# Experts stage of a two-layer metaformer: block 0's second product taken directly, and the row index worked out in block 4 instead of block 2

## The chip, the cores and the metric

The kernel runs on one core of one Trainium2 chip. Its time is the device time of one execution in microseconds (us); the time before is 2829.91 us, the median of three runs (2828.95 to 2830.11). All data is float32 unless a profile row says otherwise.

## The reference

Two layers run on 4 images of 32x32 tokens with 384 channels. Layer 0 is an attention and a mixture of experts; layer 1 is a local "outlook" attention and a feed-forward net with factored weights. The change lies in the mixture of experts:

```python
scores = jnp.einsum('bsd,de->bse', x, gate_w) + gate_b
probs = jax.nn.softmax(scores, axis=-1)
topk_vals, topk_idx = jax.lax.top_k(probs, TOP_K)      # 2 of 4 experts
...
h = jax.nn.gelu(jnp.einsum('bsd,edh->ebsh', x, w1) + b1[:, None, None, :], approximate=False)
y = jnp.einsum('ebsh,ehd->ebsd', h, w2) + b2[:, None, None, :]
out = jnp.einsum('bse,ebsd->bsd', masked, y)
```

Here x is the normed token, w1 is 384x1536 and w2 is 1536x384 for each expert. The kernel computes only the two chosen experts of each token.

## The kernel before

There are 4096 tokens and so 8192 pairs of a token and an expert. They are sorted by expert through a table in DRAM and worked in 35 blocks: blocks 0 to 3 of 256 tokens (`NFIRST` = 4), whose tokens come from the first three images, so that they can start before the last image is routed; then three short blocks, 4 to 6, of 128 tokens (`NHALF`); then blocks 7 to 34 of 256 tokens (`NLEAD` = 7 is the first of them). Every block has one expert; which expert and which tokens is worked out on the chip.

**One block** (loop at L1669). At its start GpSimd (POOL) is given the fetch of the next block's weights (`weights`, L1576: `up` of 128x4620, `down` of 128x4992) and tokens (`fetch`, L1600). There are two places for weights, so a load waits until the block two back has let go of its weights. TensorE makes 12 hidden tiles (L1693: 3 matmuls each, weights `up`, into a PSUM tile `ps_h`, three of which exist), and ScalarE takes the gelu of each (L1698). The order of hidden tiles is 0, 1, 2, 6, 7, 8, 3, 4, 5, 9, 10, 11. Then VectorE norms the next block's tokens (`norm`, L1609), and the second product follows.

**The second product** has two forms. A short block takes the direct one: 12 accumulated matmuls of 128x384 (L1715), one addition of the bias (L1720), one store of `y` to `yg`. (A float32 matmul shows as two rows of the profile, so the rows count 24.) A whole block cuts the 256x1536 by 1536x384 product into quadrants and makes it of seven products of half size instead of eight. For that VectorE makes four sums of quarters of the weights (`folded`, L1643 to L1649, at the block's start) and four sums of quarters of h (`paired`, L1656 to L1659, tiles `hsum`), one group after the hidden tile 8 and one after 11, that is after the sixth and the last of the order. The seven products (L1735) go to `ps_y` (three PSUM tiles) and are put together by nine additions of 128x192 (L1739). The third product is the first that reads `hsum`; the fourth needs a PSUM tile again. In both forms the next block's tokens are transposed on TensorE (`turn`, L1619, copied by L1620) ahead of the last part of the second product.

**What runs beside the blocks.** `beside` is a generator; each `next` puts one piece of other work into the instruction streams. It first projects the last image of the attention, one of its 8 tiles a step (L288 on TensorE, then on VectorE the addition of the residual at L760 and statistics at L763 and L764, and the store of x1 at L765; the next tile's residual load, L742, is issued ahead of it by SP, into one of two places). Then it routes that image (13 steps, with a Sqrt at L783 and an Exp at L1303 on ScalarE, and the scatter into the table on POOL at L1373), and then it runs `schedule`, L1447 on: which blocks there are, the rows of weights and tokens of all blocks (`self.all`, L1508, which blocks 4 and later need), and after that the index: where in `yg` the two results of each token lie (L1510 to L1531). The index is read by `gather` (L1540), first in block 18, where the adding up of results begins.

Steps are taken after a hidden tile's gelu: six in block 0 (those of the tiles with f % 6 >= 3), twelve each in blocks 1 and 2; what is left is taken at the start of block 3. Thus block 0 has projections 1 to 6, block 1 has projections 7 and 8 and routing, and block 2 has the end of routing (steps 19 and 20), `schedule`'s first three pieces (21 to 23), the two loops for the index (24, ahead of the first hsum group) and its last part (25, ahead of the second).

**What sets the order.** The instructions of TensorE, VectorE, ScalarE and SP stand in the order in which the program writes them (`manual_schedule`), each engine works its own list in order, and an engine that waits holds all that is behind. POOL's list is ordered by the framework's scheduler. After block 34 the outlook stage begins, whose work follows in the same lists.

Of the kernel before, what the change touches and what calls it, by code (L numbers as in the profile page):

```python
# [17 lines left out]
P = 128  # L18
# [1196 lines left out]
class Router:  # L1215
# [10 lines left out]
    def __init__(self, net, pool, keep, psum):  # L1226
        self.net, self.nc, self.tc, self.pool, self.psum = net, net.nc, net.tc, pool, psum
        nc = self.nc
        self.NJ = NT * P // XB

        def const(name, shape, dtype=FP):
            return pool.tile(shape, dtype, name=f"rt_{name}")

        def count(t, pattern, base=0, step=0):
            nc.gpsimd.iota(
                t, pattern=pattern, base=base, channel_multiplier=step, allow_small_or_imprecise_dtypes=True
            )

        self.ones = const("ones", [P, P])
        nc.gpsimd.memset(self.ones, 1.0)  # L1240
        self.before = const("before", [P, P])
        nc.gpsimd.affine_select(
            out=self.before, in_=self.ones, compare_op=ALU.is_ge, fill=0.0,
            base=-1, pattern=[[1, P]], channel_multiplier=-1,
        )
        self.lower, self.upper = const("lower", [P, NE, NE]), const("upper", [P, NE, NE])
        count(self.lower, [[1, NE], [-1, NE]])
        nc.vector.tensor_scalar(self.upper, self.lower, -0.5, None, ALU.is_lt)
        nc.vector.tensor_scalar(self.lower, self.lower, 0.5, None, ALU.is_gt)
        self.steps = const("steps", [P, self.NJ])  # L1250
        count(self.steps, [[XB, self.NJ]])
        self.number = const("number", [P, NXB])
        count(self.number[:, :NFIRST], [[UNITS, NFIRST]])
        count(self.number[:, NFIRST:NLEAD], [[1, NHALF]], base=UNITS * NFIRST)
        count(self.number[:, NLEAD:], [[UNITS, NXB - NLEAD]], base=UNITS * NFIRST + NHALF)
        self.lane = const("lane", [P, 1])
        count(self.lane, [[0, 1]], step=1)
        self.region = const("region", [P, NE])
        count(self.region, [[NT * P, NE]])

        self.next = const("next", [P, B + 2, NE])
        nc.gpsimd.memset(self.next, 1.0)
        nc.gpsimd.memset(self.next[:, :, 0:1], -float(NE - 1))
        nc.gpsimd.memset(self.next[:, 0, 0:1], 0.0)

        self.at = const("at", [P, NT, NE])
        self.sel = const("sel", [P, NT, NE])
        self.slot = [const(f"slot_{n}", [P, NT]) for n in range(2)]
        self.upto = const("upto", [P, B + 1, NE])
        nc.gpsimd.memset(self.upto[:, 0, :], 0.0)  # L1270
        self.index = [keep.tile([P, NT], mybir.dt.int32, name=f"index_{n}", tag=f"index_{n}") for n in range(2)]
        self.weight = [keep.tile([P, NT], FP, name=f"weight_{n}", tag=f"weight_{n}") for n in range(2)]
        none = const("none", [P, self.LINE], mybir.dt.int32)
        nc.gpsimd.memset(none, 0)
        n = NE * NT
        nc.sync.dma_start(
            out=net.table.rearrange("(t p) w -> p t w", p=P), in_=none.unsqueeze(1).to_broadcast([P, n, self.LINE])
        )
# [267 lines left out]
def experts(net, router, x1, x2, wup, wdown, beside):  # L1546
# [12 lines left out]
    with ExitStack() as ctx:  # L1559
# [53 lines left out]
        def turn(n):  # L1613
            xb = xbs.pop(n)
            xbT = halves[n % 2].tile([P, KC, XB], FP, name="xbT", tag="xbT")
            for t in range(tiles(n)):
                ps = router.psum()
                for c in range(KC):
                    nc.tensor.transpose(ps[:, c * P : (c + 1) * P], xb[:, t, c * P : (c + 1) * P], net.ident)  # L1619
                nc.vector.tensor_copy(  # L1620
                    xbT[:, :, t * P : (t + 1) * P], ps[:, :C].rearrange("p (c t) -> p c t", c=KC)
                )
            return xbT
# [44 lines left out]
        xbT = turn(0)  # L1668
        for n in range(NXB):  # L1669
            if n == NFIRST - 1:  # L1670
                for _ in beside:
                    pass
            if n + 1 < NXB:
                if n + 1 >= NFIRST:
                    tokens(n + 1)
                ws[n + 1] = weights(n + 1)
                fetch(n + 1)
            store()
            store = lambda: None
            if n > router.complete(added // NB):  # L1680
                store = add(added)
                added += 1
            up, down = ws.pop(n)
            size = tiles(n) * P
            whole = size == XB
            if whole:
                w11, w21, w22, t1, t2, t3, t4, shift = folded(down)
            hs, ss = [None] * NG3, []
            for f in (*range(0, 3), *range(6, 9), *range(3, 6), *range(9, 12)):
                ps = ps_h.tile([P, XB], FP, name="ps_h", tag="h")[:, :size]  # L1690
                for k in range(KC):
                    o = k * HID + f * P
                    nc.tensor.matmul(  # L1693
                        ps, lhsT=up[:, o : o + P], rhs=xbT[:, k, :size], start=k == 0, stop=k == KC - 1,
                    )
                if f % 3 == 0:
                    hs[f // 3] = hp.tile([P, 3, XB], FP, name="h", tag="h")
                nc.scalar.activation(  # L1698
                    hs[f // 3][:, f % 3, :size], ps, AF.Gelu, bias=up[:, KC * HID + f : KC * HID + f + 1]
                )  # L1700
                if n < NFIRST - 1 and (n or f % 6 >= 3):
                    next(beside, None)
                if whole and f in (8, 11):
                    g = len(ss)
                    ss.append(paired(hs[g], hs[g + 2], g))
            if n + 1 < NXB:
                norm(n + 1)
            else:
                net.scale(0, added)
            if not whole:  # L1710
                if n + 1 < NXB:
                    xbT = turn(n + 1)
                ps = ps_y.tile([P, C], FP, name="ps_y", tag="y")
                for f in range(NF):
                    nc.tensor.matmul(  # L1715
                        ps, lhsT=hs[f // 3][:, f % 3, :size], rhs=down[:, f * C : (f + 1) * C],
                        start=f == 0, stop=f == NF - 1,
                    )
                y = work.tile([P, C], FP, name="y0", tag="y0", bufs=2)
                nc.vector.tensor_tensor(y, ps, down[:, NF * C :], ALU.add)  # L1720
                nc.sync.dma_start(out=net.yg[first_row(n) : first_row(n + 1), :], in_=y)
                continue
            ys = [work.tile([P, C], FP, name=f"y{t}", tag=f"y{t}", bufs=2) for t in range(TT)]
            (c11, c12), (c21, c22) = ((y[:, :D], y[:, D:]) for y in ys)

            def a(c, t):
                return [hs[f // 3 + 2 * c][:, f % 3, t * P : (t + 1) * P] for f in range(HF)]

            def s(i):
                return [ss[f // 3][:, i, f % 3, :] for f in range(HF)]  # L1730

            def product(left, right):
                ps = ps_y.tile([P, C], FP, name="ps_y", tag="y")[:, :D]
                for f in range(HF):
                    nc.tensor.matmul(ps, lhsT=left[f], rhs=right[:, f, :], start=f == 0, stop=f == HF - 1)  # L1735
                return ps

            def total(out, one, two):
                nc.vector.tensor_tensor(out, one, two, ALU.add)  # L1739

            def send(t):
                nc.sync.dma_start(
                    out=net.yg[first_row(n) : first_row(n + 1), :].rearrange("(p t) c -> p t c", t=TT)[:, t, :],
                    in_=ys[t],
                )

            total(c21, product(a(0, 0), w11), down[:, NF * C : NF * C + D])
            total(c11, product(a(1, 0), w21), c21)
            total(c22, product(s(0), t1), shift)
            total(c21, product(s(1), t2), c21)  # L1750
            total(c12, c21, c22)
            total(c12, product(s(3), w22), c12)
            send(0)
            if n + 1 < NXB:
                xbT = turn(n + 1)
            total(c21, product(s(2), t3), c21)
            total(c22, c21, c22)
            total(c21, product(a(1, 1), t4), c21)
            send(1)
# [606 lines left out]
```

## Time and profile before

| | |
|---|---|
| median of three runs | 2829.91 us |
| profiled execution | 2827.02 us, its span 2825.3 us |
| TensorE matmul (PE) | 2615.5 us busy, 93% of the span |
| VectorE (DVE) | 1720.6 us, 61% |
| ScalarE (ACT) | 1203.6 us, 43% |
| GpSimd (POOL) | 413.8 us, 15% |
| mean granted TensorE clock | 0.959 |
| hidden tiles of the experts, L1693 | 531.8 us busy, first at 1211.6, last at 2250.2 us |
| seven products, L1735, with wsum and hsum | 205.4 us busy, 22.8 us idle before them |
| nine additions, L1739, 128x192 from PSUM | 357 ns each |

A row of a timeline gives the start, the length, the engine, the line, the operation with what it writes and reads, how many instructions are merged, and in brackets how long the engine was idle before it and what ended that. A row of merged matmuls includes the drain of the last, so the start of the next row, not the sum, tells when TensorE was free. In a row of the costliest groups, busy time and mean length in ns stand after the first bar, and idle time before the group and its releaser after the second. PEld is the load of a matmul's stationary operand, and SPq a DMA issue of SP.

### The profile page before, as it was taken

How to read it: one execution, taken by the hardware profiler on the slowest of the kernel's cores; microseconds unless marked ns; L12 is line 12 of the kernel's file. 1: busy time of each engine (PE TensorE's matmuls, PEld its weight loads, DVE VectorE, ACT ScalarE, POOL GpSimd, SP SyncE). 2: the span in 40 equal slices, each digit the busy share in tenths (PEclk: the TensorE clock that was granted, in tenths of full speed). 3: DMA queues.
4: the chain of work that ended last, by engine and by line, in shares of the span. 5: the costliest groups of instructions: out<-in, count | busy, mean ns of one | idle time of the engine just before them, and what ended most of it. 6: DMA issues, size and time to landing. Idle time of an engine off the chain costs nothing. (4 is left out here: it accounts for less than half of the span.)

```text
span 2825.3 us, 40024 instructions
## 1 busy us (share of the span) xinstructions
PE 2615.5 (93%) x14703; PEld 1570.2 (56%) x14703; DVE 1720.6 (61%) x4382; ACT 1203.6 (43%) x2023; POOL 413.8 (15%) x501
## 2 busy tenths in 40 slices
PE   6889998999999997687999999999999988999988
PEld 3323333333333332167899999999999944444432
DVE  1377777677778787657245444655555566877742
ACT  3778777678768876312222212112112122122225
POOL 1000000030003003213211112222221101100000
PEclk9999999999999998789999999999999999999999
DMA  5143434222323242453655455565665447554432
GB/s 106 31 106 90 110 92 129 75 66 72 90 60 75 68 108 58 125 204 125 248 229 208 167 208 209 210 230 210 217 224 203 156 148 217 173 178 149 147 109 91
DMA packets 215804, 404.11 MB, mean 143 GB/s; under 512 B 83344, under 2 KB 176848, under 8 KB 202544
## 3 DMA queue, kind: packets, MB, share of 16 engines
q1 hardware_dynamic: 184496, 187.82, 22.3%
q0 software_dynamic: 26960, 209.05, 21.5%
q10 hardware_dynamic: 4144, 4.61, 0.5%
q8 instruction: 118, 1.93, 0.3%
q14 instruction: 86, 0.70, 0.1%
HBM read 304.34 MB, written 49.00 MB: 125 GB/s over the span
## 5 line engine op out<-in xcount | busy, mean ns | idle before, releaser
L1698 ACT ACTIVATE h<-ps_h,up 128x256 f32<-128x256 f32 (+1 forms) x420 | 195.1, 465 | 839.7 <-PE ps_h L1693 838.8
L1693 PE MATMUL ps_h<-xbT,up 128*128 128x256 f32 (+1 forms) x2520 | 531.8, 372 | 2.5 <-ACT h L1698 1.8
L689 DVE CUSTOM_DVE_ANT_0 e<-e,rz,inv 128x1024 f32<-128x1024 f32 x384 | 475.2, 1274 | 44.6 <-DMA rz<-r_row 44.3
L1693 PEld LDWEIGHTS ps_h<-xbT,up 128*128 128x128 f32 x2520 | 463.1, 191 | 64.5 <-ACT h L1698 2.6
L637 ACT ACTIVATE e<-ps_s,ten 128x1024 f32<-128x1024 f32 x384 | 408.1, 1110 | 64.8 <-PE ps_s L627 33.1
L627 PE MATMUL ps_s<-q,k 32*128 32x512 f32 x1536 | 295.2, 673 | 44.7 <-ACT e L637 31.4
L645 PE MATMUL ps_o<-e,wv 128*32 128x512 f32 x1536 | 226.1, 663 | 50.9 <-DVE wv L696 49.4
L1735 PE MATMUL ps_y<-wsum,hsum 128*128 128x192 f32 x1152 | 205.4, 332 | 22.8 <-DVE hsum L1656 19.6
L645 PE MATMUL ps_z<-e,rt_ones 128*32 128x512 f32 x1536 | 218.3, 642 | 0.0
L716 POOL DMA_DIRECT2D q<-po x96 | 76.1, 877 | 951.5 <-DMA q<-po 560.9
L373 ACT ACTIVATE below<-tk_left,tk_bound 128x1024 bf16<-128x1024 f32 (+1 forms) x160 | 184.4, 1152 | 52.6 <-DVE tk_bound L379 40.4
L1735 PEld LDWEIGHTS ps_y<-wsum,hsum 128*128 128x128 f32 x1152 | 190.9, 193 | 27.3 <-DVE hsum L1656 21.3
L627 PEld LDWEIGHTS ps_s<-q,k 32*128 32x128 f32 x1536 | 92.5, 193 | 182.2 <-ACT e L637 90.2
L1862 PE MATMUL ps_a<-wa,xnT 128*128 128x486 f32 x384 | 169.5, 589 | 9.2 <-DVE attn L1872 7.5
L1739 DVE TENSOR_TENSOR y<-ps_y,y 128x192 f32<-128x192 f32 x160 | 57.2, 357 | 172.0 <-PE ps_y L1735 168.8
L645 PEld LDWEIGHTS ps_o<-e,wv 128*32 128x32 f32 x1536 | 31.4, 112 | 212.5 <-DVE wv L696 64.5
L288 PE MATMUL ps_t<-xnT,wqkv 128*128 128x512 f32 x288 | 135.1, 609 | 2.4 <-ACT xnT L470 1.7
L1735 PE MATMUL ps_y<-down,h 128*128 128x192 f32 x768 | 130.0, 326 | 0.0
L1735 PEld LDWEIGHTS ps_y<-down,h 128*128 128x128 f32 x768 | 126.6, 190 | 1.9
L1862 PEld LDWEIGHTS ps_a<-wa,xnT 128*128 128x128 f32 x384 | 72.3, 194 | 95.2 <-issue 85.5
L645 PEld LDWEIGHTS ps_z<-e,rt_ones 128*32 128x32 f32 x1536 | 52.2, 117 | 131.0 <-issue 127.5
L1540 POOL DMA_INDIRECT yt<-yg,index x64 | 76.7, 1198 | 323.0 <-DVE x L1835 135.3
(392 smaller groups left out, 3539.2 us busy)
## 6 DMA issues: line engine op xcount, KB each, us to landing
band<-room SPq DMA_DIRECT2D x32, 1560.0 KB
rz<-r_row SPq DMA_DIRECT2D x48, 512.0 KB
yg<-y SPq DMA_DIRECT2D x67, 192.0 KB
q<-q SPq DMA_DIRECT2D x192, 64.0 KB
k<-k SPq DMA_DIRECT2D x192, 64.0 KB
room<-none SPq DMA_DIRECT2D x64, 192.0 KB
x<-x SPq DMA_DIRECT2D x35, 192.0 KB
o<-in_x_dram SPq DMA_DIRECT2D x33, 192.0 KB
```

The lines of the kernel that those rows point to most:

```text
L288: nc.tensor.matmul(ps, lhsT=lhsT(k), rhs=rhs(k), start=k == 0, stop=k == KC - 1)
L373: nc.scalar.activation(junk[:n], left[:n], AF.Sign, bias=bound[:n], accum_out=over[:n])
L627: nc.tensor.matmul(ps[:, half * 512 : half * 512 + 512], lhsT=self.k4[r, u * P : (u + 1) * P], rhs=self.q4[r, :], start=True, stop=True,)
L637: nc.scalar.activation(e, ps, AF.Exp, bias=shift, scale=QK_SCALE)
L645: nc.tensor.matmul(ps[r : r + 32, :], lhsT=lhsT(odd), rhs=self.es[2 * u + odd][:, half * 512 : half * 512 + 512], start=u == 0, stop=u == ...
L689: nc.vector.tensor_tensor_reduce(self.es[m], self.es[m], self.rz, 1.0, self.im["inv"][:, m, self.h : self.h + 1], ALU.mult, ALU.add, self. ...
L716: nc.gpsimd.dma_start(out=there, in_=po[r : r + 32, :], accum_op=ALU.add)
L1540: self.nc.gpsimd.indirect_dma_start(out=y, out_offset=None, in_=self.net.yg[: first_row(self.complete(i // NB)), :], in_offset=bass.Indire ...
L1693: nc.tensor.matmul(ps, lhsT=up[:, o : o + P], rhs=xbT[:, k, :size], start=k == 0, stop=k == KC - 1,)
L1698: nc.scalar.activation(hs[f // 3][:, f % 3, :size], ps, AF.Gelu, bias=up[:, KC * HID + f : KC * HID + f + 1])
L1735: nc.tensor.matmul(ps, lhsT=left[f], rhs=right[:, f, :], start=f == 0, stop=f == HF - 1)
L1862: nc.tensor.matmul(pa[:, hh, :HW_], lhsT=xnT[:, k, :], rhs=wa[:, k, hh * HW_ : (hh + 1) * HW_], start=k == 0, stop=k == KC - 1,)
```

## The change

Block 0 is no longer "whole": it takes the direct product, now written for any number of 128-token tiles, with the next block's transposes ahead of the last tile. `folded` and `paired` aren't called for it. The steps of `beside` in blocks 0 to 2 are taken only while `router.all` is not there; the start of block 3 completes the steps up to it if need be; the remaining steps are taken in the short blocks, one after each hidden tile, and what is left at the start of block 7. The line numbers of functions behind the first hunk move by one, in the loop by more.

```diff
+        self.all = None
...
         for n in range(NXB):
             if n == NFIRST - 1:
+                while router.all is None:
+                    next(beside)
+            if n == NLEAD:
                 for _ in beside:
                     pass
...
-            whole = size == XB
+            whole = size == XB and n > 0
...
-                if n < NFIRST - 1 and (n or f % 6 >= 3):
+                if NFIRST <= n < NLEAD or router.all is None and n < NFIRST - 1 and (n or f % 6 >= 3):
                     next(beside, None)
...
+            out = net.yg[first_row(n) : first_row(n + 1), :].rearrange("(p t) c -> p t c", t=tiles(n))
             if not whole:
-                if n + 1 < NXB:
-                    xbT = turn(n + 1)
-                ps = ps_y.tile([P, C], FP, name="ps_y", tag="y")
-                for f in range(NF):
-                    nc.tensor.matmul(
-                        ps, lhsT=hs[f // 3][:, f % 3, :size], rhs=down[:, f * C : (f + 1) * C],
-                        start=f == 0, stop=f == NF - 1,
-                    )
-                y = work.tile([P, C], FP, name="y0", tag="y0", bufs=2)
-                nc.vector.tensor_tensor(y, ps, down[:, NF * C :], ALU.add)
-                nc.sync.dma_start(out=net.yg[first_row(n) : first_row(n + 1), :], in_=y)
+                for t in range(tiles(n)):
+                    if t == tiles(n) - 1 and n + 1 < NXB:
+                        xbT = turn(n + 1)
+                    ps = ps_y.tile([P, C], FP, name="ps_y", tag="y")
+                    for f in range(NF):
+                        nc.tensor.matmul(
+                            ps, lhsT=hs[f // 3][:, f % 3, t * P : (t + 1) * P], rhs=down[:, f * C : (f + 1) * C],
+                            start=f == 0, stop=f == NF - 1,
+                        )
+                    y = work.tile([P, C], FP, name=f"y{t}", tag=f"y{t}", bufs=2)
+                    nc.vector.tensor_tensor(y, ps, down[:, NF * C :], ALU.add)
+                    nc.sync.dma_start(out=out[:, t, :], in_=y)
                 continue
```

## The prediction

> **What bounds the kernel now.** I read the page first, then the waits of the experts stage (1211 to 2251 us), then the timelines of TensorE and VectorE around each long wait. TensorE is busy for 93% of the span, so only its gaps, or its work itself, can give time. In the costliest groups one expert row stands out by its idle time:
>
> ```profile
> L1735 PE MATMUL ps_y<-wsum,hsum 128*128 128x192 f32 x1152 | 205.4, 332 | 22.8 <-DVE hsum L1656 19.6
> ```
>
> In the stage's waits (who waited, for whom: total, times, longest) TensorE waits for hsum three times, and VectorE itself waits for residual loads:
>
> ```profile
> PE ps_y L1735 <- DVE hsum L1656: 18.4, 3, 9.8
> ...
> DVE o L760 <- DMA o<-in_x_dram: 17.2, 4, 9.2
> ```
>
> First gap, block 0, TensorE and then VectorE. The seven products begin at 1241.67, and 6.65 us pass until hsum is there. The groups of hsum are not slow: VectorE stood 9.21 us ahead of them for the residual tile of the sixth projection.
>
> ```profile
> 1241.67 4.06 PE L1735 MATMUL ps_y<-down,h 128*128 128x192 f32 x24
> 1245.57 1.14 PE L1735 MATMUL ps_y<-wsum,hsum 128*128 128x192 f32 x6
> 1253.36 2.29 PE L1735 MATMUL ps_y<-wsum,hsum 128*128 128x192 f32 x6 [6.65 <-DVE hsum L1656]
> ```
>
> ```profile
> 1251.50 0.55 DVE L760 TENSOR_TENSOR o<-o,ps_t 128x384 f32<-128x384 f32 x1 [9.21 <-DMA o<-in_x_dram]
> ...
> 1252.78 0.53 DVE L1656 TENSOR_TENSOR hsum<-h 128x384 f32<-128x384 f32 x1
> ```
>
> Second gap, block 2: here VectorE is never idle; `schedule` stands in its queue ahead of both hsum groups.
>
> ```profile
> 1318.13 4.06 PE L1735 MATMUL ps_y<-down,h 128*128 128x192 f32 x24
> 1332.01 2.29 PE L1735 MATMUL ps_y<-wsum,hsum 128*128 128x192 f32 x6 [9.82 <-DVE hsum L1656]
> 1336.25 2.29 PE L1735 MATMUL ps_y<-wsum,hsum 128*128 128x192 f32 x6 [1.95 <-DVE hsum L1656]
> ```
>
> ```profile
> 1325.81 0.18 DVE L1515 SCALAR_TENSOR_TENSOR rt_run<-rt_begun,rt_region 128x24 f32<-128x24 f32 x1
> ...
> 1331.41 0.55 DVE L1656 TENSOR_TENSOR hsum<-h 128x384 f32<-128x384 f32 x1
> ...
> 1335.65 0.55 DVE L1656 TENSOR_TENSOR hsum<-h 128x384 f32<-128x384 f32 x1
> ```
>
> From block 3 on TensorE runs without gaps, 29.85 us a whole block (2205.01 to 2234.86).
>
> **Block 0 by the direct product.** A direct tile is what a short block does: 24 matmuls of 128x384 from 1385.88 to the next work at 1393.62, 7.74 us. Two make 15.48. The seven products without a gap take 13.65 (1288.28 to 1302.59 less 0.66 of transposes), so TensorE gets 1.83 us more work. The path before is 1241.67 to 1265.58, 23.91. After: the first tile ends at 1249.41. The second stands behind block 1's transposes, and these behind norm, which VectorE does right after the same residual (nothing that sets its landing is changed up to there): norm starts at 1252.78 where hsum did, transposes follow 0.53 later (1208.88 to 1209.41 at the stage's start), the six are through by 1254.0, and the second tile by 1261.75. So the wait moves to the transposes and shrinks to 3.9 us; block 1 starts 3.8 us earlier. The removed VectorE work (fold 5.75, hsum 4.4, nine additions of 0.36, for two evictions of 0.56) lies in its idle time and is worth nothing by itself.
>
> Here a rule speaks against the change. The Trainium skill ("TensorE: Matmul & The Clock Gate", "The HAM clock gate") has the clock halved after an idle window of about 3.4 us, free-running, and restored after a busy one. The trace agrees: with work ending at 1246.7 the granted clock was 1.00 until 1251, 0.61 in that microsecond, 0.50 then, and back at about 1258, 4.7 us after work resumed: a loss of 2.3. In the other gap it fell 4.1 us after the last matmul. By the rule a 3.9 us gap can hold a whole window and would cost up to 2 us more; by the rows (4.1 and 4.5) it just misses. I take the row, zero, and keep -2.0 for the range.
>
> **Block 1.** The last residual (eighth projection) is issued by SP behind both stores of block 0, so its issue moves from 1266.58 to about 1262.9. But down of block 2 is now free only after the second eviction: POOL issues it at about 1262.5 instead of 1261.46, beside that residual instead of 5 us ahead of it. (The token fetch of block 3 can go ahead of it on POOL.) The nearest row: the sixth residual, issued 1.9 us after up of block 2, came 10.85 us after it, when the weights were through; an undisturbed one took 2.55 (1235.22 to 1237.77). Before, the DMA engines were full until 1272; the stream now begins 1 us later with two token tiles less in it, so the residual lands near 1272 (ends: 1265.5 and 1273.3). Its addition and statistics take 1.37, so ScalarE, whose Sqrt stands ahead of the next gelu and would be ready at 1271.55 (1275.36 less 3.8), starts it at 1273.4: 1.8 us late, and the 1.76 us wait of TensorE for gelu grows by that. Ends: 0 and 3.1. Net of blocks 0 and 1: 3.8 - 1.8 = 2.0.
>
> **Block 2.** Removed from VectorE's queue ahead of the first hsum: the edges and row loop, 1325.81 to 1331.41, 5.60; between the two groups: 1333.53 to 1335.65, 2.12. Counting the yields, the 23rd step sets `router.all` at the fifth hidden tile, one before the hsum, so no further step is called there. hsum then starts at 1325.81, TensorE resumes at 1326.4 instead of 1332.01, and the second wait is gone. What is late next is the fourth product, which needs a PSUM buffer: hsum groups (to 1330.0), norm 0.87, first addition 0.36, so 1331.25 against 1338.95 before: 7.7 us. The clock, cold after a gap of 4.2 us, has by then had 4.8 us to recover, so the 0.6 that twelve matmuls lost before (2.54 against 1.95) goes too, less a rest: 8.2 in all. Ends: 7.1 and 8.3.
>
> **Block 4.** All of these instructions (there are no DMAs among them) come here, on VectorE between block 3's last addition and norm of block 5: 1377.99 + 7.72 + 0.47 = 1386.2, where the transposes before ran at 1385.55 with this lead:
>
> ```profile
> 1377.51 8.20 PE L1693 MATMUL ps_h<-xbT,up 128*128 128x128 f32 x72
> 1385.55 0.49 PE L1619 MATMUL ps_t<-ident,xb 128*128 128x128 f32 x3
> 1385.88 7.91 PE L1715 MATMUL ps_y<-down,h 128*128 128x384 f32 x24
> ```
>
> So TensorE waits 0.7 us (ends 0.5 and 1.2). POOL's token request at 1378.73 waits for that norm, and up and tokens of block 6 queue behind it: 1.1 us late, but up is needed only at 1409.73, 23 us after its issue. The index is first read eighteen blocks in; nothing waits for it.
>
> **Sum.** 2.0 + 8.2 - 0.7 = 9.5 us. Everything later follows block ends and moves along. The profiled execution was 2827.02 (span 2825.3 and 1.7 around it) and would be 2817.5; the median of the runs, 2829.91, stands 2.9 above it and becomes 2820.4. A measurement of this kernel tells about 0.2% (5.7 us) from no change.
>
> **Rivals.** (a) Block 0 gives nothing: the clock falls in its 3.9 us gap (-2.0) and the residual is late; 0 to -1 there, so 8.2 - 0.7 - 0.7 = 6.8, 2823.1. For it: the rule, and the 9 us that the sixth residual took. Against: both rows of the clock. (b) The residual is in time: 3.8 + 8.2 - 0.7 = 11.3, 2818.6. For it: it is issued almost with the weights. (c) The wait moves: in block 2 something else, such as block 3's tokens for norm or the short blocks' weights, holds what hsum held; under 5 us, about 2827. Against: that norm ran at once after hsum before. (d) Slower: from 1388 to 1432 the DMA engines were 0.73 to 1.02 full with three blocks' weights, about 345 GB/s. If up of block 6, 1.1 us late into a full stream, came only when that stream ends, 22 us after block 6 wants it (1432 less 1409.7), the price would outweigh the 9.5: 2842. It decides from a delay of about 15 us (the load takes some 8 of its 23) plus the gain; the shown delay is 1.1.
>
> **Chances.** Forecast 0.52, (a) 0.20, (b) 0.16, (c) 0.09, (d) 0.03. The likeliest gives 2820.4. Best ends: 3.8 + 8.3 - 0.5 = 11.6, 2818.3; worst: 0.2 + 7.1 - 1.2 = 6.1, 2823.8, and 1 us each way for the runs and for a cold clock in block 1: 2817.3 to 2825.0. Faster 0.86 (forecast, (b), most of (a)), same 0.11, slower 0.03.
>
> **What would show it.** Block 0: two runs of 24 matmuls of 128x384 with about 3.9 us between, granted clock 1.00 between; block 1's first matmul near 1261.8. Block 1: VectorE waiting for the residual about 2 us, TensorE for gelu about 3.5. Block 2: one wait for hsum of about 4.2, none between the groups. Block 4: transposes 0.7 late, waiting for norm. Wrong if the wait in block 2 stays near 10, if short blocks gain gaps ahead of L1693 or L1715, or if block 4's transposes come more than 1.5 late.

## The result and the profile after

The changed kernel took 2817.52 us (median of 6 runs, 2810.71 to 2821.45). Beside it the kernel before took 2831.16 (6 runs, 2828.95 to 2837.16): a ratio of 0.9947, 95% interval 0.9931 to 0.9963, some 15 us. Applied to the 2829.91 that the prediction started from, this is 2814.9: below the forecast's 2820.4 and below its range, which began at 2817.3 (the median as it stands, 2817.52, lies 0.2 inside it). The gain is some 15 us by the ratio, 13.6 between the two medians and 15.4 in the traces below, where 9.5 were forecast and 11.6 was the best case. The profiled execution took 2810.71 us (span 2809.0); the one before took 2827.02.

In the page's groups, the row of the seven products has 36 matmuls fewer and its idle time fell from 22.8 to 9.9 us:

```profile
L1741 PE MATMUL ps_y<-wsum,hsum 128*128 128x192 f32 x1116 | 198.9, 332 | 9.9 <-DVE hsum L1657 6.7
```

In the waits of the same stage (1208 to 2240) TensorE waits for hsum once, 4.4 us, instead of three times:

```profile
PE ps_y L1741 <- DVE hsum L1657: 4.4, 1, 4.4
```

Block 0 on TensorE's timeline. The two direct tiles have nothing but six transposes between them; the forecast had drawn a gap of 3.9 us there:

```profile
1239.58 7.90 PE L1721 MATMUL ps_y<-down,h 128*128 128x384 f32 x24
1247.32 0.82 PE L1620 MATMUL ps_t<-ident,xb 128*128 128x128 f32 x6
1247.97 7.91 PE L1721 MATMUL ps_y<-down,h 128*128 128x384 f32 x24
1255.71 1.46 PE L1697 MATMUL ps_h<-xbT,up 128*128 128x256 f32 x6
```

The reason stands on VectorE's timeline. The sixth residual, for which VectorE stood 9.21 us before, is added at 1241.97 after a wait of 1.88, and norm (L1610) follows while the first tile is still running:

```profile
1241.97 0.56 DVE L760 TENSOR_TENSOR o<-o,ps_t 128x384 f32<-128x384 f32 x1 [1.88 <-DMA o<-in_x_dram]
...
1243.25 0.83 DVE L1610 TENSOR_SCALAR xb<-xb,ids 128x384 f32<-128x384 f32 x2
```

Blocks 2 and 4 went as drawn. In block 2 one wait for hsum of 4.40 is left, and a small one for an addition:

```profile
1308.26 4.06 PE L1741 MATMUL ps_y<-down,h 128*128 128x192 f32 x24
1316.72 4.00 PE L1741 MATMUL ps_y<-wsum,hsum 128*128 128x192 f32 x12 [4.40 <-DVE hsum L1657]
1321.61 2.22 PE L1741 MATMUL ps_y<-wsum,hsum 128*128 128x192 f32 x12 [0.88 <-DVE y L1745]
```

Block 4's transposes wait 0.74 for norm, behind the steps that came there:

```profile
1368.63 0.52 PE L1620 MATMUL ps_t<-ident,xb 128*128 128x128 f32 x3 [0.74 <-DVE xb L1610]
```

To compare two executions I count from block 0's first transposes (1209.41 before, 1207.93 after), and read where each block's first matmul stands:

| | before | after | change | forecast |
|---|---|---|---|---|
| block 1 begins | 56.17 | 47.78 | -8.39 | -3.8 |
| block 1 is long | 37.01 | 37.01 | 0 | +1.8 |
| block 2 is long | 45.40 | 37.45 | -7.95 | -8.2 |
| block 4, the first short one with steps, is long | 16.11 | 17.04 | +0.93 | +0.7 |
| block 7 begins | 216.75 | 201.34 | -15.41 | -9.5 |

Up to block 7 the four terms give the whole difference. Behind it single blocks differ by up to 1.1 us here and there, in both directions.

### The profile page after: what moved, and what is told of

It reads as the page before. It is cut to its first block, busy times and chain, and to the rows that moved or that the text cites. A ratio compares the mean times of both kernels' runs of the same rounds, so it can differ in the third digit from the quotient of the medians.

```text
span 2809.0 us, 39930 instructions
## 1 busy us (share of the span) xinstructions
PE 2618.3 (93%) x14667; PEld 1565.4 (56%) x14667; DVE 1710.4 (61%) x4362; ACT 1203.0 (43%) x2023; POOL 415.3 (15%) x501
## 3 DMA queue, kind: packets, MB, share of 16 engines
q8 instruction: 118, 1.93, 0.3%
## 5 line engine op out<-in xcount | busy, mean ns | idle before, releaser
L1741 PE MATMUL ps_y<-wsum,hsum 128*128 128x192 f32 x1116 | 198.9, 332 | 9.9 <-DVE hsum L1657 6.7
L1741 PEld LDWEIGHTS ps_y<-wsum,hsum 128*128 128x128 f32 x1116 | 185.2, 194 | 13.6 <-DVE hsum L1657 8.0
```

## The experiments

"Block 1 at" and "block 7 at" are counted as in the table. Ratios are to runs of the kernel before on the same chip; runs of any of these kernels scatter by some 5 us about their median, single ones by up to 17, so the shape in the trace decides, and the ratio goes beside it. A trace shows one execution of each run.

**One part at a time.** The direct product alone, with the index steps back in block 2:

```diff
-                while router.all is None:
-                    next(beside)
-            if n == NLEAD:
...
-                if NFIRST <= n < NLEAD or router.all is None and n < NFIRST - 1 and (n or f % 6 >= 3):
+                if n < NFIRST - 1 and (n or f % 6 >= 3):
```

> Block 0 takes the direct product; the index stays in block 2. Theory A (a race): whether the sixth residual of block 0 lands 2 us or 9 us after VectorE asks for it is decided by about 1 us, by whether its load is issued before or after the stream of block 2's up has begun, and the direct product has no part in it. Then VectorE's wait is either about 2 or about 9 here too; with 2, block 0's second product takes 16.1 us from its first matmul to block 1's (8.4 less than in the trace of before, but 1.8 more than seven products would take with the residual early), with 9 about 20 (3.8 less). Block 2 keeps its waits for hsum of 9.8 and 2 us. Time: 2 to 8 us under before. Theory B (the direct product itself makes the residual early): the wait is about 2 us, always, and the time 8 us under before.

Measured: 2825.41, ratio 0.9981 (0.9969 to 0.9993). Block 1 at 47.78, block 7 at 208.50 (8.25 earlier than before); block 2 keeps its 9.77 and 1.95 us waits. The residual was early (wait 1.43).

The move alone, with seven products in block 0:

```diff
-            whole = size == XB and n > 0
+            whole = size == XB
```

> Only the index moves to block 4; block 0 keeps its seven products. Both theories: block 2 gains about 8 us (one wait for hsum of 4.4 us in place of 9.8 and 2), block 4 loses 0.7 to 0.9. Theory A: block 0's wait for hsum is 6.6 us or nearly none, as the race falls, so the time is 7 us under before, and as much as 16 under it where the residual is early. Theory B: block 0's wait stays at 6.6 us and the time is 7 us under before.

Measured: 2823.39, ratio 0.9962 (0.9943 to 0.998). Block 1 at 55.58, block 7 at 208.91 (7.84 earlier). The residual was late, as before:

```profile
1254.23 0.56 DVE L760 TENSOR_TENSOR o<-o,ps_t 128x384 f32<-128x384 f32 x1 [8.76 <-DMA o<-in_x_dram]
```

So the parts add up to within 0.7 us (8.25 and 7.84 against 15.41), and the surplus belongs to the direct product: of these runs, the residual comes in time only in those with it.

**Is it the residual?** Before, a residual tile has two places in SBUF, so the load of the sixth waits until the store of the fourth has landed. Four places in the kernel before take that wait away:

```diff
-                o = late[0].tile([P, C], FP, name="o", tag="o", bufs=2)
+                o = late[0].tile([P, C], FP, name="o", tag="o", bufs=4)
```

> The kernel before with four places for the residual tiles instead of two, so that a residual load no longer waits until a store has landed; its sixth is issued about 3 us earlier, ahead of the stream of block 2's up. Theory A: VectorE's wait of 9.2 us is gone (under 3), block 0's second product runs without a gap, 14.3 us with the transposes instead of 23.9: 9.6 us under before without any direct product. Theory B, or a load that is slow because the DMA engines are full whenever it is issued: the wait stays at 6 to 9 us and the time within 3 us of before.

Measured: 2821.98, ratio 0.9959 (0.9944 to 0.9975). The residual's wait is 1.70, block 0's seven products run without a gap, block 1 begins at 46.04 and block 7 at 207.70. That is 10.1 us earlier than 56.17: the whole gap in block 0 was the residual's.

The changed kernel once more:

> The changed kernel once more, for a second look at the race and for the size of the gain on this chip. Theory A: VectorE's wait for the sixth residual may be about 9 us this time; then block 0 is 3.8 us shorter than in the first trace of before instead of 8.4. Theory B: about 2 us again. Time 10 to 16 us under before.

Measured: 2815.46, ratio 0.9929 (0.9913 to 0.9946). Early again: wait 1.50, block 1 at 47.57, block 7 at 200.90.

**What does the direct product do for the residual?** It drops block 0's four weight sums on VectorE. They are put back at the block's start, as extra work whose result nothing uses:

```diff
-            if whole:
+            if size == XB:
                 w11, w21, w22, t1, t2, t3, t4, shift = folded(down)
```

> The changed kernel, but VectorE still makes the four weight sums of block 0 at its start, and nothing reads them. Theory B1 (the sums, not the products, made the residual late: while VectorE makes them, POOL's issue of block 1's up takes 1.89 us instead of 1.05, the two weight loads start up to 0.8 us later, the third residual behind them too, and the sixth residual then loses its race against block 2's up): that issue takes 1.9 us again, VectorE waits about 9 us for the sixth residual, TensorE about 4 us ahead of block 1's transposes, and the time rises by 4 to 6 us over the changed kernel. Theory B2 (hsum or the seven products themselves make it late): the issue takes 1.05, the wait is about 2 us, the time is that of the changed kernel.

Measured: 2820.65, ratio 0.9957 (0.994 to 0.9974). Residual late (8.84), block 1 at 53.48, block 7 at 208.45. TensorE's timeline is the picture that the prediction had drawn:

```profile
1240.99 7.90 PE L1721 MATMUL ps_y<-down,h 128*128 128x384 f32 x24
1252.78 1.24 PE L1620 MATMUL ps_t<-ident,xb 128*128 128x128 f32 x6 [3.88 <-DVE xb L1610]
1253.81 9.30 PE L1721 MATMUL ps_y<-down,h 128*128 128x384 f32 x24
```

How the sums reach the residual is seen on POOL and VectorE. In the kernel before, POOL's request for block 1's up takes 1.89 us while VectorE works at the sums; first POOL, then VectorE:

```profile
1215.77 1.89 POOL L1576 DMA_INDIRECT up<-in_wup_dram,rows_w_first  x1 [0.30 <-issue]
```

```profile
1214.12 1.35 DVE L1645 TENSOR_TENSOR wsum<-down 128x1152 f32<-128x1152 f32 x1
1215.39 1.35 DVE L1646 TENSOR_TENSOR wsum<-down,wsum 128x1152 f32<-128x1152 f32 x1
```

In the changed kernel it takes 1.04:

```profile
1214.19 1.04 POOL L1577 DMA_INDIRECT up<-in_wup_dram,rows_w_first  x1 [0.30 <-issue]
```

The request waits out the addition that it falls into: 0.97 us of L1646's were left when it began, and it ended 0.92 us after that addition. So it is in all twenty profiles: each request for up, down or tokens that began with 0.2 us or more of such an addition left ended 0.81 to 0.92 us after it, whether 0.2 or 1.19 us were left. The Trainium skill ("SBUF — State Buffer", "SBUF: two separate sides") says that GpSimd, which writes the descriptors of DMAs in POOL's queue, shares a port pair with VectorE, and that in some cases, a VectorE operation with two inputs in SBUF against a GpSimd operation that reads SBUF among them, whichever comes second waits for the other's whole instruction. The wait to the addition's end agrees; but the same page ("Who interferes with whom") has `tensor_tensor`, the operation of these additions, not stalling a DMA in its own probe, and there the numbers here decide. That it is this lock no run here parts from another cause. Everything behind the request starts some 0.9 us later (the one for down 8.55 us after the first transposes instead of 7.61), and with it the residual chain: the third addition stands at 24.1 to 24.5 without the sums (six profiles, of two places or four), at 24.8 to 25.5 with them at the block's start (eleven).

Then the sums were kept, but held back until block 0's second gelu, in the move-only kernel:

```diff
+                if n == 0 and f == 1:
+                    mark = work.tile([P, 1], FP, name="mark", tag="mark", bufs=1)
+                    nc.vector.tensor_copy(mark, hs[0][:, 1, 0:1])
+                    fold = folded(down)
```

> The index in block 4 and seven products in block 0, but the four weight sums of block 0 start only after its second gelu (a copy of one element holds them), some 6 us later, when POOL has issued block 1's loads. Theory B1: the issue of up takes about 1.05 us, the sixth residual comes within 2 us, block 0's second product has no gap (14.3 us), and the time is 9 us under the kernel with the index alone moved, and 2 us under the changed one. Theory B2: VectorE's wait stays near 9 us and TensorE's wait for hsum near 6.6.

Measured: 2812.47, ratio 0.9941 (0.9919 to 0.9962). The request took 1.04, the residual was early (1.96), block 1 at 46.74, block 7 at 200.30.

> A second look at the kernel with the index in block 4, seven products in block 0 and the weight sums begun after the second gelu. If POOL's issue of up decides, it again takes about 1.05 us, VectorE waits about 2 us for the sixth residual, and block 1 starts about 46.7 us after the first transposes, 1 us ahead of the changed kernel; if the first look was luck, the wait may be 9 us. Time 15 to 17 us under before.

Measured: 2814.13, ratio 0.9949 (0.9932 to 0.9966): the other way. The request again took 1.04, but the residual was late (8.62), block 1 at 54.49, block 7 at 208.87. The sums had only moved their weight: a later request on POOL, for tokens, took 2.01 us beside them, 1.72 in the first run. So one program has both outcomes, and the request for up alone doesn't decide.

**What the direct product costs by itself.** With four places the residual is early in either form:

```diff
-                o = late[0].tile([P, C], FP, name="o", tag="o", bufs=2)
+                o = late[0].tile([P, C], FP, name="o", tag="o", bufs=4)
```

> The index in block 4, seven products in block 0, four places for residual tiles. Both theories: no gap in block 0 and 4.2 us in block 2; 9.6 + 8 - 0.9 = 17 us under before, about 2 us under the changed kernel.

> The changed kernel with four places for residual tiles: what the direct product costs where the residual is early anyway. Both theories: block 0's second product 16.1 us against 14.3 in the run beside it, block starts 1.8 us later; time 1.8 us over it, equal to the changed kernel.

Measured: seven products and the move 2817.85, ratio 0.9956 (0.994 to 0.9972), block 1 at 45.72, block 7 at 199.33; direct product and the move 2814.66, ratio 0.9936 (0.9911 to 0.9961), block 1 at 47.83, block 7 at 201.18. The direct product is 1.85 to 2.1 us longer, as its matmuls say (forecast 1.83). By the clock the two can't be told apart.

Then the first of these, with a step after only the first hidden tile of each short block:

```diff
-                if NFIRST <= n < NLEAD or router.all is None and n < NFIRST - 1 and (n or f % 6 >= 3):
+                if NFIRST <= n < NLEAD and f == 0 or router.all is None and n < NFIRST - 1 and (n or f % 6 >= 3):
```

> The index in the short blocks, but one step a block (its two loops beside block 4, its last part beside block 5), seven products in block 0, four places for residual tiles. Theory: norm of block 5 then waits for 5.6 us of index work instead of 7.7 and is done before TensorE wants the transposes, so the wait of 0.73 us in block 4 goes and none comes in block 5. From the first transposes to block 7: 0.9 us less than with both steps in block 4 (198.4 against 199.3), 2.9 less than in the changed kernel. Time 17 to 18 us under before; that it is under the changed kernel too lies within what the runs scatter.

Measured: 2813.40, ratio 0.9953 (0.9936 to 0.997). Block 4's 0.73 us wait is gone, but block 7 begins at 200.36 instead of the expected 198.4, because block 2 took 39.35 us instead of 37.67. None of these is shown to be faster than the changed kernel: all the intervals overlap its own.

**What decides the race?** I had seen that the late profiles had under 2.05 us from the fourth tile's store to POOL's request for block 2's up, a stream of 2.4 MB. A pause on POOL ahead of that request was to part them:

```diff
+                if n == 1:
+                    pause = work.tile([P, XB], FP, name="pause", tag="pause", bufs=1)
+                    nc.gpsimd.tensor_copy(pause, last)
```

> The kernel before, with one small copy on POOL between block 0's last gelu and the request for up of block 2 (it reads that gelu's tile, so it can't run sooner). Nothing else is changed: weight sums at the start of block 0, two places for the residual tiles, the index in block 2. Theory (the sixth residual loses its race when up of block 2 is requested less than some 2.05 us after the store ahead of it): the copy makes that gap about 2.5 to 3 us, so the residual's load follows its store after about 2.6 us instead of 3.9, VectorE waits under 3 us instead of 9.2, block 1 begins about 47 us after block 0's transposes instead of 56, and block 7 at about 208.5 instead of 216.75: the time 8 us less. Rival (the loads are late for a cause of their own, up's request doesn't matter): the residual's wait stays at 8 to 9 us, block 1 at 56, and the time as before.

> The move alone, seven products in block 0 and weight sums at its start, with the same small copy on POOL ahead of up of block 2. Theory: the residual is early though the sums are where they were, block 1 at about 46.5 instead of 55.6 and block 7 at about 200.3 instead of 208.9, as with the sums held back when that won the race. Rival: residual late, block 7 at about 209 as with the move alone. If the pause were to cost anything itself, it is up of block 2 that comes about 0.7 us later, 30 us before block 2 wants it.

Measured, on a chip on which the kernel before took 2870.84: 2869.92, ratio 1.0 (0.9983 to 1.0017), and 2863.25, ratio 0.9965 (0.995 to 0.9979). Residual late in both (8.32 and 9.09). The copy took only 0.39 us; the distances were 1.98 and 2.28. Six copies:

```diff
-                    nc.gpsimd.tensor_copy(pause, last)
+                    for _ in range(6):
+                        nc.gpsimd.tensor_copy(pause, last)
```

> The kernel before with six small copies on POOL between block 0's last gelu and the request for up of block 2, since one copy put the request off by only some 0.4 us (0.39 of work) and moved nothing. Six hold it back by some 2.5 us and more, so the gap from the fourth tile's store to that request is about 4 us instead of 2.0. Theory (the sixth residual's load races the 2.4 MB stream): the load follows its store after 2.5 to 2.7 us instead of 3.9, VectorE waits about 2 us for it instead of 9.2, block 1 begins about 46 us after block 0's transposes instead of 56, and block 7 at about 208 instead of 216.75. Rival (the stream has nothing to do with it): residual late by 8 to 9 us, block 1 near 56.

> The move alone with the same six copies. Theory: residual early, block 1 at about 46 instead of 55.6, block 7 at about 200 instead of 208.9, though the weight sums stand at the start of block 0. Rival: as the move alone.

Measured: 2830.00, ratio 1.0027 (1.0012 to 1.0043), and 2818.86, ratio 0.9983 (0.9965 to 1.0). In both programs five of the six copies ended up behind the request, so the distances were 2.23 and 2.45, not 4, and both were late (9.02 and 9.21). The second speaks against a distance of 2.05 as the point of decision: the direct product alone was early at the same 2.45.

Next, POOL was held back ahead of block 1's up in the changed kernel, without any sums:

```diff
+                if n == 0:
+                    pause = work.tile([P, XB], FP, name="pause", tag="pause", bufs=1)
+                    for _ in range(2):
+                        nc.gpsimd.tensor_copy(pause, ws[0][0][:, :XB])
```

> The changed kernel with two small copies on POOL ahead of the request for up of block 1, no weight sums in block 0: they hold POOL back by about 0.8 to 1.2 us there, as the sums on VectorE did by lengthening that request from 1.04 to 1.89. Theory (the sums acted on the residuals only by holding POOL back): the third residual's addition comes at 25.3 or later instead of 24.5, the fourth tile's store later, the sixth residual is late by about 8.8 us, TensorE waits some 3.9 us ahead of block 1's transposes, block 1 begins at about 53.5 instead of 47.8, block 7 at 208 instead of 201. Rival (the sums acted in another way, such as VectorE's own time): residual early, block 1 at 47.8, block 7 at 201.

Measured: 2819.10, ratio 0.9977 (0.996 to 0.9994). The request came 2.8 us later than in the changed kernel, a larger dose than meant: the copy ahead of it took 0.40 us, but first waited 2.40 for an earlier transfer of POOL's. Third addition at 26.90, residual late, block 1 at 54.03, block 7 at 208.67:

```profile
1254.27 0.55 DVE L760 TENSOR_TENSOR o<-o,ps_t 128x384 f32<-128x384 f32 x1 [7.89 <-DMA o<-in_x_dram]
```

A later POOL is enough to lose the race; VectorE's own time isn't needed.

> The changed kernel once more, on the chip of these runs, for the shape of block 0: if the race is what the theory says, the sixth residual is early (wait under 2.5 us) and block 1 begins at about 47.8, block 7 at about 201, as in its two profiles so far; a late one would show that the sums removed make it likely only.

Measured: 2816.61, ratio 0.9974 (0.9956 to 0.9992). Early a third time: wait 1.54, block 1 at 48.31, block 7 at 202.91.

The DMA queues showed another candidate: a packet of 0.02 MB in the queue called instruction, one in some 30 us here. In the move with six copies it falls into the fourth tile's store (0.25 us from 1.20 behind its issue):

```profile
q1 hardware_dynamic: 68, 0.09, 101.7%
q8 instruction: 1, 0.02, 25.9%
```

In the direct product alone it comes when the store is through (0.25 us from 2.17):

```profile
DMA packets 1, 0.02 MB, mean 66 GB/s; under 512 B 0, under 2 KB 0, under 8 KB 0
...
q8 instruction: 1, 0.02, 23.0%
```

The Trainium skill ("Runtime: NRT & Kernel Launch", "Instruction fetch mechanics") has programs fetched in blocks of 256 instructions, 16 KiB, mostly hidden. The page of the kernel before fits: this queue has 118 packets, 1.93 MB, for TensorE's 29,406 rows, one for every 249. If the packet is TensorE's program, 16 or 8 more of its instructions at the kernel's start would move it by about 2.2 or 1.1 us (24 records in 3.25 us there). Four extra matmuls in the kernel before, two in the changed one, their result overwritten at once:

```diff
+            for _ in range(4):
+                nc.tensor.matmul(ps[:, :NE], lhsT=router.ones, rhs=gates[:, 0, :], start=True, stop=True)
```

> The kernel before with four matmuls of 128x4 more at the kernel's start, some 1,200 us ahead of the experts; their result is overwritten by the matmuls that follow, and nothing after them is changed. The trace counts two passes a matmul and a weight load for each, so TensorE's program is 16 instructions longer ahead of block 0. New theory: the fourth tile's store is late because a fetch of TensorE's program[...] falls into the middle of it. In the six late profiles in which it was looked up the packet comes 1.0 to 1.5 us after the store's issue, in the five early ones 1.75 to 2.25. Block 0 takes 24 of these records in 3.25 us, so 16 instructions bring the fetch 2.2 us forward, from 1.5 us after the store's issue to 0.7 ahead of it, where no tile moves. Expected: the load follows its store after 2.5 to 2.7 us instead of 3.9, VectorE waits about 2 us for the sixth residual instead of 9.2, block 1 begins about 46 us after block 0's transposes instead of 56, block 7 at about 208, with weight sums, order and every transfer of the kernel where they were. Rival (the race with the request for up of block 2): nothing moves, residual late, block 1 at 56, block 7 at 216.75.

> The changed kernel with two such matmuls more at the kernel's start: eight instructions, 1.1 us, which bring the fetch from 1.75 to 2.25 us after the fourth tile's store to 0.7 to 1.2 after it, into its middle. New theory: the store lands late, the load follows after 3.6 to 3.9 us, the sixth residual is waited for about 8.5 us, TensorE waits 3.9 us ahead of block 1's transposes, block 1 begins at about 53.5 instead of 47.8 and block 7 at about 208 instead of 201: the changed kernel loses what it gained beyond the forecast. Rival: as the changed kernel, early.

Measured: 2827.46, ratio 0.9996 (0.9979 to 1.0014), late (8.78), block 1 at 56.64, block 7 at 217.79; and 2818.86, ratio 0.9957 (0.9942 to 0.9972), early (1.50), block 1 at 48.72, block 7 at 203.74. But the packet didn't go where it was sent: 1.6 us behind the store in the first (1.7 in the kernel before), 2.2 in the second. So the count of instructions doesn't set its place as I thought, and these two runs don't test the packet as a cause.

All profiles with two places, by four distances in us: from the third addition to block 0's first product, from the fourth tile's store to block 2's up request, to that packet, and to the sixth residual's load.

| kernel | addition to product | store to up | store to packet | store to load | VectorE's wait |
|---|---|---|---|---|---|
| POOL held back, no sums | 6.01 | 1.63 | 1.1 | 3.70 | 7.89 |
| before, 4 matmuls more | 6.31 | 1.32 | 1.6 | 4.00 | 8.78 |
| before, one copy | 6.35 | 1.98 | 1.3 | 3.92 | 8.32 |
| direct with sums | 6.38 | 1.39 | 1.4 | 3.69 | 8.84 |
| move alone | 6.45 | 1.50 | 1.4 | 3.84 | 8.76 |
| before, six copies | 6.64 | 2.23 | 1.4 | 3.72 | 9.02 |
| move, one copy | 6.71 | 2.28 | 1.3 | 3.58 | 9.09 |
| late sums, second run | 6.74 | 1.78 | 1.5 | 4.00 | 8.62 |
| move, six copies | 6.77 | 2.45 | 1.4 | 3.62 | 9.21 |
| before | 6.92 | 1.99 | 1.7 | 3.86 | 9.21 |
| after | 7.12 | 2.10 | 1.9 | 2.69 | 1.88 |
| after, second | 7.21 | 2.32 | 2.3 | 2.52 | 1.50 |
| late sums | 7.31 | 2.35 | 2.1 | 2.70 | 1.96 |
| direct alone | 7.44 | 2.45 | 2.3 | 2.55 | 1.43 |
| after, third | 7.70 | 2.85 | 2.0 | 2.51 | 1.54 |
| after, 2 matmuls more | 8.34 | 3.32 | 2.2 | 2.69 | 1.50 |

The first column parts late from early without exception, at about 7.0: how far the residual chain runs ahead of TensorE. The store to packet column does so too (1.7 and less, 1.9 and more), store to up does not. With a later load everything follows: it then runs beside up's 2.4 MB and arrives some 8 us later.

What makes the store land late can be read from its single packets. In the move alone the store is issued at 1241.95. The first row below is the stretch from 1243.30 to 1243.40, in which the instruction packet begins; its 65.1% of 16 engines in 0.1 us are 1.04 us of one. From 1244.20 to 1244.40 (second row) no packet begins at all. From 1244.40 to 1245.30 (last two) the rest of the store follows in SP's queue q1, eight packets of data and a small one that closes:

```profile
q8 instruction: 1, 0.02, 65.1%
...
DMA packets 0, 0.00 MB, mean 0 GB/s; under 512 B 0, under 2 KB 0, under 8 KB 0
...
DMA packets 21, 0.23 MB, mean 260 GB/s; under 512 B 1, under 2 KB 9, under 8 KB 9
...
q1 hardware_dynamic: 9, 0.01, 6.3%
```

It is so in nine of the ten late profiles: the last eight (in one the last four) of the store's 256 data packets start where the instruction packet ends, the first of them within 0.02 us of it; in the tenth, the kernel before, only the closing packet does. A store ends with sixteen counts on its semaphore. Fifteen are there by 2.65 us behind the issue in all sixteen profiles; the last comes by then in the six early ones and at 3.5 to 3.95 in the ten late ones, and the load follows it by 0.05 us. With four places the packet falls into the fifth store, whose last count comes 0.8 to 1.9 us behind the others in four profiles of four, but no load waits for it. So one sixteenth of the store waits behind the packet. The packet goes by TensorE's place, roughly: it begins 0.7 to 2.1 us ahead of block 0's first product in all sixteen. Weight sums or a pause on POOL shift the residual chain against that. This is read from the packets' times; no run moved the packet alone.

## Why the prediction was wrong, step by step

- **Block 0's product.** Right: 16.13 us from the first direct matmul to block 1's (1239.58 to 1255.71), forecast 15.48 and 0.66 of transposes.
- **Block 0's wait: the step that failed.** "Nothing that sets its landing is changed up to there", and the removed VectorE work "lies in its idle time and is worth nothing by itself". The weight sums lay in VectorE's idle time but beside POOL's request. Taking them off let the residual chain run some 0.8 us earlier, so that the fourth tile's store was all but through when the instruction packet came, and that wins a race worth 8 to 9 us. With the sums in place at the block's start the residual was late in eight profiles of eight, without them it was early in the changed kernel, both its repeats, the one with two matmuls more and the direct product alone, and the pause on POOL makes it late without them. The gap of 3.9 us was worked out rightly for a late residual (3.88 measured with the sums) and wasn't there: -8.39 instead of -3.8.
- **The clock.** With no gap in block 0 it had nothing to fall in: 1.00 at 1241 to 1243 and at 1250 to 1253. That the term of zero came true is luck, for the row was chosen wrongly against the rule, as the direct product with sums shows, where the gap of 3.88 us was there (stretches of 1 us, with the granted clock third from the end):

```profile
1252.00:1253.00 1.00, 0.23 (x2) 0.26 (x3) 0.96 (x5) 0.00 (x0) 0.00 (x0) 1.00 0.56 117
1253.00:1254.00 1.00, 1.00 (x7) 0.92 (x6) 0.95 (x3) 0.00 (x0) 0.00 (x0) 0.60 0.75 277
1254.00:1255.00 1.00, 1.00 (x3) 0.48 (x2) 0.56 (x1) 0.00 (x0) 0.71 (x1) 0.50 0.53 197
```

  The clock fell to 0.50 and the second tile took 9.30 us instead of 7.90: 1.4 us lost where zero was taken. With POOL held back it fell even in a gap of 3.17 (0.53 from 1256 to 1257; 8.90). So the 4.1 and 4.5 us of the kernel before were no lower bound. The trace's clock records show why: between two changes lies always a multiple of 3.41 us (34.13, 6.83, 68.27 and 13.65 us in the kernel before, 37.55, 3.41 and 68.27 with the sums), so the clock falls at the next tick of a window that runs freely. That agrees with the Trainium skill's window of about 3.4 us ("TensorE: Matmul & The Clock Gate", "The HAM clock gate"), only that the window need not be idle throughout: with the sums it fell at 1253.20, 0.4 us after work had resumed, and with POOL held back at 1256.06, 3.1 us after the last matmul, by ends of matmuls that the profile models.
- **Block 1.** Forecast +1.8, measured 0: TensorE's wait for gelu is 1.77 against 1.76. The last residual was issued at 1256.91, 0.17 us behind POOL's request for down of block 2, which took 1.81 beside block 1's weight sums, and was added at 1263.14 without a wait. The lower end, 0, was the right one; that the request itself would be slow was not seen.
- **Block 2.** 7.95 for 8.2. hsum's wait is 4.40 (forecast 4.2). The fourth product came 7.47 us earlier after the first (forecast 7.7; its wait of 0.88 for an addition was in the sum), and what follows it was 0.48 shorter (forecast 0.5). But none of this is as firm as the numbers look: the changed kernel's two repeats took 37.22 and 38.62 us for block 2, and the longer had a second wait for hsum of 0.72, which the forecast had excluded.
- **Block 4.** 0.93 for 0.7: the wait 0.74 as forecast.
- **Rivals.** (b) had the residual of block 1 in time and came nearest, 11.3. (a), (c) and (d) left no trace: no clock loss, no new wait in the short blocks' weights. All had the 3.9 us gap or less gain in block 0 in them, so the range could not reach 15. Its other end was not consistent either: the worst case took 0.2 for blocks 0 and 1, where (a) has 0 to -1.

In the sum: 8.39 + 0 + 7.95 - 0.93 = 15.41, where 3.8 - 1.8 + 8.2 - 0.7 = 9.5 stood. Shown by experiment is that block 0's surplus is the sixth residual's, that holding POOL back loses it and four places secure it. That the fourth store lands late because part of it waits for the instruction packet is read from the packets' times, and what sets the packet's exact place stays open.

## What to carry to other kernels

Idle time on an engine doesn't make work there free: look at what other queues do in that very microsecond, above all POOL's DMA requests beside large VectorE operations. Where a wait of 9 us stands behind a load that is normally back in 2.6, it is a race with a margin, so ask how far from its edge it stands, and what in the change moves either runner by half a microsecond. A second buffer pair (two places to four) took that race away with no cost that stands out of the traces, and is safer than winning it by 0.2 us. And when one of a transfer's sixteen parts lands late, look for what it stood behind: the program's own fetches are transfers too.

## What the runs showed of the hardware

- A POOL indirect DMA request for weights or tokens took 0.94 to 1.05 us around block 0 when no VectorE addition of 128x1152 fp32, both operands in SBUF, was under way; begun with 0.2 us or more of one left it ended 0.81 to 0.92 us after the addition, and so took up to 1.89 (up), 1.82 (down) or 2.01 (tokens).
- A store of 192 KB whose last packets met an instruction packet of 0.9 to 1.3 us got the last of its sixteen counts at 3.5 to 3.95 us behind its issue in ten profiles; where the packet began 1.9 us or more behind the issue, at 2.65 or less in six.
- A load of 192 KB issued 2.5 to 2.7 us behind that store was added 2.4 to 2.9 us after its issue; issued 3.6 to 4.0 us behind it, beside a 2.4 MB indirect load, 7.6 to 9.1.
- The granted clock changed only at multiples of 3.41 us within an execution, in all twenty profiles, and so fell at very different distances from the last matmul: 2.67 us in block 2 of the move with four places, 5.39 in block 2 of the changed kernel with two matmuls more.
- One and the same program, the late sums, began block 1 at 46.74 in one execution and at 54.49 in another, with the residual chain 0.57 us nearer to TensorE's place.
